# Moving elementwise work between VectorE, ScalarE and GpSimd in a four-layer graph network

## The chip, the cores and the metric

The kernel runs on one core of a Trainium2 chip. A core has a matrix engine (TensorE, "PE" in the profile, its weight loads "PEld"), a vector engine (VectorE, "DVE"), a scalar engine (ScalarE, "ACT"), a third elementwise engine (GpSimd, "POOL") and a queue engine for transfers (SyncE, "SP"). They run side by side, each in the order of its own queue, and wait for each other by semaphores. Matmul results land in PSUM, which has eight banks here, each of 128 partitions by 512 numbers of fp32; everything else lies in SBUF. The metric is the time of the whole kernel on the device, in microseconds (us), as the median of several runs.

## The reference

There are 128 graphs of 64 nodes with 256 features. Four layers follow each other, each of the form `x = layernorm(x + layer(x, adj))`. What matters here is layer 0 (a gated network of five steps), layer 1 (an RMS norm over 1024 hidden features) and the layer norm that closes each layer:

```python
def _layernorm(x, axis=-1, eps=1e-5):
    m = jnp.mean(x, axis=axis, keepdims=True)
    v = jnp.var(x, axis=axis, keepdims=True)
    return (x - m) / jnp.sqrt(v + eps)

# layer 0: five gated steps
for l in range(weight.shape[0]):
    m = jnp.einsum('bnd,de->bne', h, weight[l])
    agg = jnp.einsum('bij,bid->bjd', A, m)
    h = _gru_cell(agg, h, w_ih, w_hh, b_ih, b_hh)      # r, z, n gates, then (1 - z) * n + z * h

# layer 1: hidden features with an RMS norm
agg = epsilon * x + neighbor_sum
h = jnp.einsum('bnd,dh->bnh', agg, W1) + b1
var = jnp.mean(jnp.square(h), axis=-1, keepdims=True)
h = jax.nn.silu(h * jax.lax.rsqrt(var + eps) * rms_weight)
out = jnp.einsum('bnh,hd->bnd', h, W2) + b2
# layers 2 and 3: a hyperbolic map and an attention over adj
```

## The kernel before

The kernel works on 16 groups of 8 graphs. Two graphs share the 128 partitions, so a group is four blocks (`NB = 4`) of 128 rows. Three groups' buffers exist (`NF = 3`), and a small list scheduler written in Python interleaves the groups: each operation is recorded with an engine, an expected duration and what it reads and writes, and is then issued in an order that keeps the engines busy under those durations. The scheduler runs while the program is built; on the chip each engine just works down its queue. All of it is fp32, and the trace shows each fp32 matmul of the program as two instructions (transposes as one).

One gated step works on the group's two halves `n = 0, 1`, each 128 partitions by 2 x 256. It uses the differences between the halves, so that the products of the second half are built from those of the first:

```python
def aggregate(dst, src, b0, n):
    ps = bank("ps_agg")
    for j in range(2):
        for c in range(KD):
            pe(128, lambda j=j, c=c: matmul(ps[...], src[:, b0 + j, ...], ed[:, 2 * n + j, :], 0, 1), ...)
    act(512, lambda: nc.scalar.copy(dst[:, :, half(n)], blocks_of(ps.tile())), [(dst, n)], [ps])   # L476

def minus(o, x0, x1, r):                                                                           # L550
    pool(1.32, lambda: nc.gpsimd.tensor_sub(view(o), x0(), x1()), [o], r)

def plus(o, ps, x):                                                                                # L567
    dve(512, lambda: nc.vector.tensor_add(o.tile(), blocks_of(ps.tile()), x.tile()), [o], [ps, x])

def new_n(n, t):
    # L580: t = (t + 1) * hnb          two inputs in SBUF
    # L582: t = p_in + t               one input in PSUM
    # L584: t = tanh(t + bias)         ScalarE
    # L586: hN = h - t                 two inputs in SBUF
def new_state(n, t, z):
    # L590: hN = (z + 1) * hN          L592: hN = 0.5 * hN + t      two inputs in SBUF each

sides(0)                         # aggregate(agg, hr, 0, 0), p_hn, hnb of half 0
... cut: products p1 and p_in of half 0, its gate and new_n(0, ur) ...
sides(1)                         # the same of half 1
minus(t1, of(a, 1), of(a, 0), [a])                                # t1 = agg1 - agg0
minus(t2, of(h, 1), lambda: view(t1), [(h, 1), t1])               # t2 = h1 - t1
minus(t3, of(h, 1), of(a, 1), [(h, 1), (a, 1)])                   # t3 = h1 - agg1
minus(t4, lambda: view(t2), of(h, 0), [t2, (h, 0)])               # t4 = t2 - h0
product(pu, s2[l], k_view(t2), True, True, t2);  plus(uu, pu, uu)
product(pv, s3[l], k_view(t3), True, False, t3); plus(uv, pv, uu)
product(pw, s1[l], k_view(t1), True, False, t1)
product(pv, na22, k_view(t4), False, True, t4)
plus(uv, pw, uv)
plus(uz, pv, uu)
... cut: the gates' tanh, new_state(0), new_n(1), new_state(1) ...
```

`t1` and `t2` are the two halves of a tile that the trace calls tA, `t3` and `t4` those of tB; `a` is the aggregate in SBUF (agg in the trace), `h` the state (hT), and `uu`, `uz`, `uv`, `ur` are the tiles U, Z, V, R. The matmuls of `product` have line L482 in the trace, those of `aggregate` and of the later layers L222.

A layer norm collects statistics on VectorE, takes the power -0.5 on GpSimd and scales on VectorE:

```python
def layer_norm(y, tag, name):
    for b in range(NB):
        # L491, L492: bn_stats, bn_aggr of block b into mv (mean, variance)       VectorE
    pool(0.23, ... ve = variance + LN_EPS ...)                                    # L493
    pool(1.04, ... rstd = ve ** -0.5 ...)                                         # L494
    for b in range(NB):
        dve(256, lambda b=b: nc.vector.tensor_scalar(                             # L497
            o[:, b, :], y[:, b, :], mv[:, b, 0:1], rstd[:, b:b + 1], OP.subtract, OP.mult), ...)
```

Layer 1 computes its 1024 hidden features in eight blocks of 128 features by 512 rows, and sums their squares:

```python
for c in range(KH):                                               # 8 blocks
    ps = bank("ps_hid")
    ... cut: two matmuls of 512 columns into ps (L222) ...
    act(512, ... hc = ps + b1 ...)                                # L668, out of PSUM
    pool(1.04, ... sq = hc * hc ...)                              # L671, GpSimd
    if c:
        dve(512, ... sqs = sqs + sq ...)                          # L674
... cut: ps_ss, the power on GpSimd (L681), ps_rms, the gate (L689 to L694), ps_o, layer norm ...
```

Of the kernel before, what the change touches and what calls it, by code (L numbers as in the profile page):

```python
# [14 lines left out]
OP = mybir.AluOpType  # L15
# [134 lines left out]
def kernel(  # L150
# [79 lines left out]
    def dve(n, run, w, r):  # L230
        flow.op("DVE", 0.16 + 0.00105 * n, run, w, r)

    def act(n, run, w, r):
        flow.op("ACT", 0.27 + 0.00077 * n, run, w, r)

    def pool(us, run, w, r=()):
        flow.op("POOL", us, run, w, r)
# [8 lines left out]
    def blocks_of(t):  # L246
        return t.rearrange("p (b d) -> p b d", d=D)
# [175 lines left out]
    def b1c(c):  # L423
        return cols[:, 2 * NV + c:2 * NV + c + 1]
# [7 lines left out]
    def group(g):  # L432
# [9 lines left out]
        def rows(tag, name):  # L442
            return u(tag, name, (P, NB, D))

        def half(n):
            return slice(n * HR, (n + 1) * HR)
# [21 lines left out]
# [5 lines that stand above are left out]
                    pe(128, lambda j=j, c=c: matmul(  # L473
                        ps[:, c * HR + j * P:c * HR + (j + 1) * P], src[:, b0 + j, c * P:(c + 1) * P],
                        ed[:, 2 * n + j, :], 0, 1), [ps], [(src, b0 + j), ed])
            act(512, lambda: nc.scalar.copy(dst[:, :, half(n)], blocks_of(ps.tile())), [(dst, n)], [ps])  # L476

        def product(ps, w, v, first, last, r):

# [7 lines left out]
        def layer_norm(y, tag, name):  # L487
            st, mv = tiny("st", (P, NB, 6)), tiny("mv", (P, NB, 2))
            ve, rstd = tiny("ve"), tiny("rstd")
            for b in range(NB):  # L490
                dve(256, lambda b=b: nc.vector.bn_stats(st[:, b, :], y[:, b, :]), [(st, b)], [(y, b)])  # L491
                dve(4, lambda b=b: nc.vector.bn_aggr(mv[:, b, :], st[:, b, :]), [(mv, b)], [(st, b)])  # L492
            pool(0.23, lambda: nc.gpsimd.tensor_scalar(ve.tile(), mv[:, :, 1], LN_EPS, None, OP.add), [ve], [mv])  # L493
            pool(1.04, lambda: nc.gpsimd.tensor_tensor(rstd.tile(), ve.tile(), m_half, OP.pow), [rstd], [ve])  # L494
            o = rows(tag, f"x_{name}")
            for b in range(NB):
                dve(256, lambda b=b: nc.vector.tensor_scalar(  # L497
                    o[:, b, :], y[:, b, :], mv[:, b, 0:1], rstd[:, b:b + 1], OP.subtract, OP.mult),
                    [(o, b)], [(y, b), mv, rstd])
            return o  # L500

        if g >= 2:
# [18 lines left out]
        def gated(l, h):  # L521
            agg = u("agg", f"agg{l}", (P, KD, R))
            hr = rows("B", f"hr{l}") if l else xt

            hnb = u("y", f"hnb{l}", (P, KD, R))

            def sides(n):

                if l:
                    ps = rows_of(h, n)  # L530
                    act(512, lambda: nc.scalar.copy(hr[:, 2 * n:2 * n + 2, :], blocks_of(ps.tile())),
                        [(hr, 2 * n), (hr, 2 * n + 1)], [ps])
                aggregate(agg, hr, 2 * n, n)
                p_hn = bank("p_hn")
                product(p_hn, w_hn, lambda k: h[:, k, half(n)], True, True, (h, n))
                for c in range(KD):
                    act(300, lambda c=c: nc.scalar.activation(  # L537
                        hnb[:, c, half(n)], p_hn[:, c * HR:(c + 1) * HR], AF.Identity,
                        bias=half_b[:, 2 * KD + c:2 * KD + c + 1], scale=0.5), [(hnb, (n, c))], [p_hn, half_b])

            hN = u("h", f"hT{l}", (P, KD, R))
            tA, tB = (u(i, f"t{i}_{l}", (P, 2 * KD, HR)) for i in "AB")
            t1, t2, t3, t4 = (tA, 0), (tA, 1), (tB, 0), (tB, 1)
            a = agg

            def view(t):
                return t[0][:, t[1] * KD:(t[1] + 1) * KD, :]

            def minus(o, x0, x1, r):
                pool(1.32, lambda: nc.gpsimd.tensor_sub(view(o), x0(), x1()), [o], r)  # L550

            def of(t, n):
                return lambda: t[:, :, half(n)]

            def k_of(t, n):
                return lambda k: t[:, k, half(n)]

            def k_view(t):
                return lambda k: t[0][:, t[1] * KD + k, :]

            p1, pu, pv, pw = bank("p_r0"), bank("p_u"), bank("p_v"), bank("p_w")
            p_in = [bank("p_in"), bank("p_in")]

            uu, uz, uv, ur = (u(t, f"{t}_{l}", (P, KD, HR)) for t in ("ZUVR" if l % 2 else "UZVR"))

            def plus(o, ps, x):
                dve(512, lambda: nc.vector.tensor_add(o.tile(), blocks_of(ps.tile()), x.tile()), [o], [ps, x])  # L567

            def tanh_half(o, src, i, r):
                for c in range(KD):  # L570
                    act(256, lambda c=c: nc.scalar.activation(  # L571
                        o[:, c, :], src(c), AF.Tanh, bias=half_b[:, i * KD + c:i * KD + c + 1], scale=0.5),
                        [(o, c)], [r, half_b])

            def inplace(o):
                return lambda c: o[:, c, :]

            def new_n(n, t):

                dve(512, lambda: nc.vector.scalar_tensor_tensor(  # L580
                    t.tile(), t.tile(), 1.0, hnb[:, :, half(n)], OP.add, OP.mult), [t], [t, (hnb, (n, 0)), (hnb, (n, 1))])
                dve(512, lambda: nc.vector.tensor_add(t.tile(), blocks_of(p_in[n].tile()), t.tile()), [t], [t, p_in[n]])  # L582
                for c in range(KD):
                    act(256, lambda c=c: nc.scalar.activation(t[:, c, :], t[:, c, :], AF.Tanh, bias=bih(2 * KD + c)),  # L584
                        [(t, c)], [(t, c), cols])
                dve(512, lambda: nc.vector.tensor_sub(hN[:, :, half(n)], h[:, :, half(n)], t.tile()), [(hN, n)], [(h, n), t])  # L586

            def new_state(n, t, z):

                dve(512, lambda: nc.vector.scalar_tensor_tensor(  # L590
                    hN[:, :, half(n)], z.tile(), 1.0, hN[:, :, half(n)], OP.add, OP.mult), [(hN, n)], [(hN, n), z])
                dve(512, lambda: nc.vector.scalar_tensor_tensor(  # L592
                    hN[:, :, half(n)], hN[:, :, half(n)], 0.5, t.tile(), OP.mult, OP.add), [(hN, n)], [(hN, n), t])

            sides(0)
            product(p1, a11[l], k_of(a, 0), True, False, (a, 0))
            act(420, lambda: nc.scalar.copy(uu.tile(), blocks_of(p1.tile())), [uu], [p1])
            product(p_in[0], w_in[l], k_of(a, 0), True, True, (a, 0))
            product(p1, a12, k_of(h, 0), False, True, (h, 0))
            tanh_half(ur, lambda c: p1[:, c * HR:(c + 1) * HR], 0, p1)  # L600
            new_n(0, ur)
            sides(1)

            minus(t1, of(a, 1), of(a, 0), [a])
            minus(t2, of(h, 1), lambda: view(t1), [(h, 1), t1])
            minus(t3, of(h, 1), of(a, 1), [(h, 1), (a, 1)])
            minus(t4, lambda: view(t2), of(h, 0), [t2, (h, 0)])
            product(pu, s2[l], k_view(t2), True, True, t2)  # L610
            plus(uu, pu, uu)
            product(pv, s3[l], k_view(t3), True, False, t3)
            plus(uv, pv, uu)
# [4 lines that stand above are left out]
            product(pw, s4[l], k_of(h, 1), False, True, (h, 1))  # L618
            tanh_half(uz, inplace(uz), 1, uz)
            new_state(0, ur, uz)  # L620
            tanh_half(uv, inplace(uv), 1, uv)
            plus(uu, pw, uu)
            product(p_in[1], w_in[l], k_of(a, 1), True, True, (a, 1))
            tanh_half(uu, inplace(uu), 0, uu)
            new_n(1, uu)
            new_state(1, uu, uv)
            return hN
# [34 lines left out]
        for c in range(KH):  # L662
            ps = bank("ps_hid")
            for k in range(KD):
# [3 lines left out]
            act(512, lambda ps=ps, hc=hc, c=c: nc.scalar.activation(  # L668
                hc[0][:, hc[1], :], ps.tile(), AF.Identity, bias=b1c(c)), [hc], [ps, cols])
            sq = u("ZR"[c % 2], f"sq{c}") if c else sqs  # L670
            pool(1.04, lambda hc=hc, sq=sq: nc.gpsimd.tensor_mul(sq.tile(), hc[0][:, hc[1], :], hc[0][:, hc[1], :]),  # L671
                 [sq], [hc])
            if c:
                dve(512, lambda sq=sq: nc.vector.tensor_add(sqs.tile(), sqs.tile(), sq.tile()), [sqs], [sqs, sq])  # L674
        ps = bank("ps_ss")
# [190 lines left out]
```

## Time and profile before

The median of three runs is 2712.8 us (2710.44 to 2714.72). One profiled execution had a span of 2704.5 us:

| engine | busy, us | share | instructions |
|---|---|---|---|
| PE (matmul) | 2488.3 | 92% | 11970 |
| DVE | 1675.7 | 62% | 3594 |
| ACT | 1079.3 | 40% | 2371 |
| POOL | 780.8 | 29% | 707 |

The profile gives the busy time of each engine, the waits (an idle stretch before an instruction is put down to the instruction whose end released it), the chain that ended last (followed back from the last instruction, at each step to what released it) and the single instructions in order of time. The end of a matmul is modelled and matmuls overlap in the array, so a busy PE need not be a PE at its peak; the distance between starts says more. The granted TensorE clock is 0.979 of full speed in the mean and lower in the last part of the run, where the last group has the core to itself.

The groups of instructions that the change touches, before:

| line, engine | what | count | mean, ns |
|---|---|---|---|
| L550 POOL | the four differences, 128x512 | 80 each | 1348 to 1465 |
| L671 POOL | squares of a hidden block, 128x512 | 112, and 16 into sqs | 1039, 1088 |
| L497 DVE | scaling of a layer norm, 128x256 | 192 and 64 | 483, 438 |
| L476 ACT | copy of the aggregate out of PSUM, 128x512 | 160 | 578 |
| L668 ACT | hidden block out of PSUM, 128x512 | 128 | 687 |

### The profile page before, as it was taken

Reading aid. Unit: us, or ns where it says so; the run is one execution under the profiler, and the core shown is the slowest. Engines: PE = TensorE matmul, PEld = TensorE weight load, DVE = VectorE, ACT = ScalarE, POOL = GpSimd, SP = SyncE. Lnnn points to the kernel's source line nnn. Section 1 sums busy time; section 2 is a strip of 40 time slices with the busy share of each in tenths; the row PEclk is TensorE's granted clock in tenths of the full one; section 3 lists DMA queues with packets and bytes.
Section 4 is the critical chain, followed back from the end, with each engine's and each line's share of the span. In section 5 each row is a group of like instructions: output and inputs, shape, how many; then the busy total and the mean of one; then the engine's idle time right before and its main releaser. Section 6 shows DMA issues by size and latency. Waiting matters only on the chain.

```text
span 2704.5 us, 32558 instructions
## 1 busy us (share of the span) xinstructions
PE 2488.3 (92%) x11970; PEld 2059.1 (76%) x11970; DVE 1675.7 (62%) x3594; ACT 1079.3 (40%) x2371; POOL 780.8 (29%) x707
## 2 busy tenths in 40 slices
PE   7999998999999899998999989999999999999874
PEld 5887877788787777877788777877777778787743
DVE  2456766676566656656576566765667566576635
ACT  3444433444434344433444334444334443434322
POOL 4224133322413323133322323233233322323220
PEclk9999999999999999999999999999999999999986
DMA  3000000000000000000000000000000000000000
GB/s 116 1 9 1 18 9 15 12 1 26 0 18 8 1 26 1 19 8 18 8 1 26 1 18 8 18 9 1 18 9 18 9 1 26 1 9 8 3 13 8
DMA packets 39150, 35.16 MB, mean 13 GB/s; under 512 B 9892, under 2 KB 38592, under 8 KB 38992
## 3 DMA queue, kind: packets, MB, share of 16 engines
q1 hardware_dynamic: 34848, 28.05, 3.2%
q10 hardware_dynamic: 3744, 4.46, 0.5%
q8 instruction: 95, 1.56, 0.2%
q0 software_dynamic: 400, 0.57, 0.1%
q14 instruction: 63, 0.52, 0.1%
HBM read 24.69 MB, written 8.39 MB: 12 GB/s over the span
## 4 chain that ended last, share of the span: by engine, by line
PE 56%; DVE 21%; POOL 10%; issue 6%; ACT 6%; DMA 0%; POOLq 0%; DVEq 0%; ACTq 0%; SPq 0%
PE ps_hid L222 8%; PE p_v L482 7%; PE ps_o L222 7%; PE p_r L482 7%; PE p_w L482 5%; PE p_in L482 5%; POOL tA L550 4%; PE ps_agg L222 3%; PE p_hn L482 3%; POOL tB L550 3%; PE p_u L482 3%; DVE st L491 2%; PE ps_a L222 2%; DVE x_n L497 2%; DVE hT L590 2%
## 5 line engine op out<-in xcount | busy, mean ns | idle before, releaser
L550 POOL TENSOR_TENSOR tA<-agg 128x512 f32<-128x512 f32 x80 | 107.8, 1348 | 841.9 <-ACT agg L476 738.7
L482 PE MATMUL p_hn<-hT,w_hn 128*128 128x256 f32 x1280 | 323.6, 381 | 0.0
L482 PE MATMUL p_in<-agg,w_in 128*128 128x256 f32 x1280 | 312.5, 380 | 7.6 <-ACT agg L476 7.6
L482 PEld LDWEIGHTS p_in<-agg,w_in 128*128 128x128 f32 x1280 | 241.0, 190 | 41.3 <-ACT agg L476 9.7
L482 PEld LDWEIGHTS p_hn<-hT,w_hn 128*128 128x128 f32 x1280 | 230.0, 192 | 23.7
L222 PE MATMUL ps_o<-w2s,hid 128*128 128x256 f32 x1024 | 231.5, 381 | 3.7 <-DVE hid L694 3.4
L222 PE MATMUL ps_hid<-aggm,w1s 128*128 128x512 f32 x512 | 224.7, 597 | 0.7 <-ACT aggm L476 0.7
L571 ACT ACTIVATE V<-V,half_b 128x256 f32<-128x256 f32 x160 | 73.2, 501 | 377.5 <-DVE V L567 377.5
L222 PEld LDWEIGHTS ps_o<-w2s,hid 128*128 128x128 f32 x1024 | 194.5, 191 | 33.0 <-DVE hid L694 6.3
L482 PE MATMUL p_u<-tA,s 128*128 128x256 f32 x640 | 162.5, 393 | 44.3 <-POOL tA L550 44.2
L674 DVE TENSOR_TENSOR sqs<-sqs,sq 128x512 f32<-128x512 f32 x112 | 77.5, 692 | 180.0 <-POOL sq L671 180.0
L222 PEld LDWEIGHTS ps_hid<-aggm,w1s 128*128 128x128 f32 x512 | 97.7, 192 | 118.2 <-issue 114.4
L482 PE MATMUL p_v<-tB,na 128*128 128x256 f32 x640 | 163.9, 396 | 25.1 <-DVE V L567 24.8
L482 PEld LDWEIGHTS p_u<-tA,s 128*128 128x128 f32 x640 | 119.4, 194 | 78.1 <-POOL tA L550 60.9
L482 PE MATMUL p_w<-tA,s 128*128 128x256 f32 x640 | 162.6, 381 | 0.0
L482 PEld LDWEIGHTS p_v<-tB,na 128*128 128x128 f32 x640 | 123.6, 198 | 50.4 <-DVE V L567 16.8
L482 PE MATMUL p_r<-agg,a 128*128 128x256 f32 x640 | 156.1, 381 | 6.1 <-ACT agg L476 6.0
L482 PE MATMUL p_r<-hT,a 128*128 128x256 f32 x640 | 159.4, 379 | 0.0
L537 ACT ACTIVATE hnb<-p_hn,half_b 128x256 f32<-128x256 f32 x320 | 134.2, 469 | 62.5 <-PE p_hn L482 61.3
L482 PE MATMUL p_w<-hT,s 128*128 128x256 f32 x640 | 159.0, 380 | 0.0
L580 DVE SCALAR_TENSOR_TENSOR R<-R,hnb 128x512 f32<-128x512 f32 x80 | 65.0, 812 | 143.7 <-ACT R L571 143.3
L482 PE MATMUL p_v<-tB,s 128*128 128x256 f32 x640 | 153.9, 379 | 0.0
(192 smaller groups left out, 4932.5 us busy)
## 6 DMA issues: line engine op xcount, KB each, us to landing
x<-in_x_dram SPq DMA_DIRECT2D x16, 512.0 KB, 3.7
xr<-in_x_dram SPq DMA_DIRECT2D x16, 512.0 KB, 3.3
out_dram<-x_n SPq DMA_DIRECT2D x16, 512.0 KB, 2.9
edge<-in_adj_dram SPq DMA_DIRECT2D x32, 64.0 KB, 2.3
wm<-in_L_gnn_weight_dram ACTq DMA_DIRECT2D x5, 256.0 KB, 8.9
w1s<-in_L_gnn_W_dram ACTq DMA_DIRECT2D x1, 1024.0 KB, 11.7
w2s<-in_L_gnn_W_dram ACTq DMA_DIRECT2D x1, 1024.0 KB, 8.4
aw_in_L_gnn_w_ih_dram<-in_L_gnn_w_ih_dram ACTq DMA_DIRECT2D x1, 512.0 KB, 5.6
```

Source lines behind the costliest of these rows:

```text
L222: nc.tensor.matmul(o, lhsT, rhs, start=(k == 0), stop=(k == nk - 1))
L482: pe(256, lambda c=c, k=k: nc.tensor.matmul(ps[:, c * HR:(c + 1) * HR], w[:, k, c * P:(c + 1) * P], v(k), start=first and c == k == 0, sto ...
L491: dve(256, lambda b=b: nc.vector.bn_stats(st[:, b, :], y[:, b, :]), [(st, b)], [(y, b)])
L497: dve(256, lambda b=b: nc.vector.tensor_scalar(o[:, b, :], y[:, b, :], mv[:, b, 0:1], rstd[:, b:b + 1], OP.subtract, OP.mult), [(o, b)], [ ...
L537: act(300, lambda c=c: nc.scalar.activation(hnb[:, c, half(n)], p_hn[:, c * HR:(c + 1) * HR], AF.Identity, bias=half_b[:, 2 * KD + c:2 * K ...
L550: pool(1.32, lambda: nc.gpsimd.tensor_sub(view(o), x0(), x1()), [o], r)
L571: act(256, lambda c=c: nc.scalar.activation(o[:, c, :], src(c), AF.Tanh, bias=half_b[:, i * KD + c:i * KD + c + 1], scale=0.5), [(o, c)], ...
L580: dve(512, lambda: nc.vector.scalar_tensor_tensor(t.tile(), t.tile(), 1.0, hnb[:, :, half(n)], OP.add, OP.mult), [t], [t, (hnb, (n, 0)), ( ...
L590: dve(512, lambda: nc.vector.scalar_tensor_tensor(hN[:, :, half(n)], z.tile(), 1.0, hN[:, :, half(n)], OP.add, OP.mult), [(hN, n)], [(hN, ...
L674: dve(512, lambda sq=sq: nc.vector.tensor_add(sqs.tile(), sqs.tile(), sq.tile()), [sqs], [sqs, sq])
```

## The change

Three kinds of elementwise work change engines. The differences of the gated steps go from GpSimd to VectorE, and the two that use the second half's aggregate read it from its PSUM bank rather than from the copy that ScalarE makes. The squares of layer 1 go from GpSimd to ScalarE, which reads the hidden block's PSUM bank a second time (the square of the same sum with the bias). Of each layer norm's four scalings two go from VectorE to ScalarE, as `rstd * y + off`, for which VectorE computes `off = -mean * rstd` in one small instruction. GpSimd keeps the powers, a bias sum per group and little else. The purpose is to take GpSimd out of the gated steps' path and to use idle ScalarE time. The scheduler's expected durations change with it, so the order of instructions changes on every engine.

```diff
@@ aggregate, sides
+            return ps                       # aggregate hands out its bank
-                aggregate(agg, hr, 2 * n, n)
+                p_agg = aggregate(agg, hr, 2 * n, n)
+                return p_agg                # so does sides
@@ layer_norm
+            off = tiny("off")
+            dve(4, lambda: nc.vector.scalar_tensor_tensor(
+                off.tile(), mv[:, :, 0], -1.0, rstd.tile(), OP.mult, OP.mult), [off], [mv, rstd])
             for b in range(NB):
-                dve(256, lambda b=b: nc.vector.tensor_scalar(
-                    o[:, b, :], y[:, b, :], mv[:, b, 0:1], rstd[:, b:b + 1], OP.subtract, OP.mult),
-                    [(o, b)], [(y, b), mv, rstd])
+                if b % 2:
+                    act(300, lambda b=b: nc.scalar.activation(
+                        o[:, b, :], y[:, b, :], AF.Identity, bias=off[:, b:b + 1], scale=rstd[:, b:b + 1]),
+                        [(o, b)], [(y, b), off, rstd])
+                else:
+                    dve(240, lambda b=b: nc.vector.tensor_scalar(
+                        o[:, b, :], y[:, b, :], mv[:, b, 0:1], rstd[:, b:b + 1], OP.subtract, OP.mult),
+                        [(o, b)], [(y, b), mv, rstd])
@@ gated
             def minus(o, x0, x1, r):
-                pool(1.32, lambda: nc.gpsimd.tensor_sub(view(o), x0(), x1()), [o], r)
+                dve(512, lambda: nc.vector.tensor_sub(view(o), x0(), x1()), [o], r)
...
-            sides(1)
+            p_a2 = sides(1)
+            a2 = lambda: blocks_of(p_a2.tile())
-            minus(t1, of(a, 1), of(a, 0), [a])
+            minus(t1, a2, of(a, 0), [p_a2, (a, 0)])
             minus(t2, of(h, 1), lambda: view(t1), [(h, 1), t1])
-            minus(t3, of(h, 1), of(a, 1), [(h, 1), (a, 1)])
+            minus(t3, of(h, 1), a2, [(h, 1), p_a2])
             minus(t4, lambda: view(t2), of(h, 0), [t2, (h, 0)])
@@ layer 1
             sq = u("ZR"[c % 2], f"sq{c}") if c else sqs
-            pool(1.04, lambda hc=hc, sq=sq: nc.gpsimd.tensor_mul(sq.tile(), hc[0][:, hc[1], :], hc[0][:, hc[1], :]),
-                 [sq], [hc])
+            act(512, lambda ps=ps, sq=sq, c=c: nc.scalar.activation(sq.tile(), ps.tile(), AF.Square, bias=b1c(c)),
+                [sq], [ps, cols])
```

## The prediction

> **What bounds the kernel now.** I read the page's first part, then the chain, then the waits of TensorE, then stretches of the run, and last one stretch instruction by instruction.
>
> The page (time in us, share of the span, number of instructions; the second line is the chain that ended last, by engine):
>
> ```profile
> PE 2488.3 (92%) x11970; PEld 2059.1 (76%) x11970; DVE 1675.7 (62%) x3594; ACT 1079.3 (40%) x2371; POOL 780.8 (29%) x707
> PE 56%; DVE 21%; POOL 10%; issue 6%; ACT 6%; DMA 0%; POOLq 0%; DVEq 0%; ACTq 0%; SPq 0%
> ```
>
> TensorE is the bound. How far from its own limit is it? Its "busy" is too generous, because the ends of matmuls are modelled, so I take the distance from start to start in runs without a gap. In the chain, 40 matmuls of ps_o (256 columns) take 8.65 us, 0.216 each; 32 of ps_hid (512 columns) take 13.73 to 13.9, 0.433 each; 128 columns or a transpose come to half of 0.216, 0.108. Counted by shape in the grouped instructions there are 552 of 512 columns, 8616 of 256 or 257 and 2802 small ones: 239 + 1864 + 304 = 2407 us. Of the span of 2704.5 some 297 us is therefore not matmul streaming, and no change on the other engines can win more than that. Where does it lie? Stretches of the run (length; busy us and count of each engine; TensorE clock; DMA):
>
> ```profile
> 0.00:100.00 100.00, 85.60 (x404) 68.34 (x405) 30.71 (x57) 33.53 (x79) 38.57 (x43) 1.00 0.25 78
> 1000.00:1400.00 400.00, 375.45 (x1795) 310.64 (x1794) 250.91 (x538) 163.35 (x359) 122.03 (x109) 0.99 0.03 9
> 2500.00:2600.00 100.00, 83.54 (x380) 69.25 (x378) 59.25 (x149) 33.46 (x79) 22.20 (x22) 0.93 0.03 11
> 2600.00:2705.00 105.00, 55.25 (x176) 37.35 (x176) 48.98 (x148) 21.52 (x44) 18.93 (x22) 0.70 0.02 5
> ```
>
> Priced as above, the first 100 us lose 18 (10 of them the first loads), the last 205 us lose about 90, because the last group of molecules runs almost alone, and 100 to 2500 loses about 190 in many small gaps. The gaps by what ended them (us in total, times, longest):
>
> ```profile
> PE p_u L482 <- POOL tA L550: 44.2, 37, 3.6
> PE ps_hr L463 <- DVE hT L592: 27.4, 18, 4.5
> PE p_v L482 <- DVE V L567: 24.8, 19, 4.2
> PE ps_sup L222 <- DVE tan L743: 24.1, 7, 9.9
> PE ps_agg L222 <- DVE x_n L497: 18.9, 16, 3.8
> ```
>
> The largest is the wait of p_u for the difference t2 that GpSimd makes; the next four are waits for VectorE results. Now the same stretch on GpSimd and on VectorE (start, duration, instruction):
>
> ```profile
> 1059.62 1.27 POOL L550 TENSOR_TENSOR tA<-agg 128x512 f32<-128x512 f32 x1 [4.90 <-ACT agg L476]
> 1060.85 1.72 POOL L550 TENSOR_TENSOR tB<-hT,agg 128x512 f32<-128x512 f32 x1
> 1062.53 1.72 POOL L550 TENSOR_TENSOR tA<-hT,tA 128x512 f32<-128x512 f32 x1
> ```
>
> ```profile
> 1058.37 0.69 DVE L580 SCALAR_TENSOR_TENSOR R<-R,hnb 128x512 f32<-128x512 f32 x1
> 1059.70 1.74 DVE L580 SCALAR_TENSOR_TENSOR R<-R,hnb 128x512 f32<-128x512 f32 x1
> 1061.54 0.69 DVE L582 TENSOR_TENSOR R<-p_in,R 128x512 f32<-128x512 f32 x1
> 1062.15 2.65 DVE L586 TENSOR_TENSOR hT<-hT,R 128x512 f32<-128x512 f32 x2
> ```
>
> The same L580 takes 0.69 us while GpSimd is idle and 1.74 us beside a GpSimd subtraction; L582, which has one input in PSUM, keeps its 0.69. GpSimd's subtractions stretch too, from 1.27 to 1.72.
>
> **What the Trainium skill says.** "SBUF — State Buffer", section "Who interferes with whom": a VectorE instruction with two SBUF inputs shares a read path with GpSimd instructions that read SBUF, and whichever issues second fully blocks. The trace agrees. Adding up, for each VectorE form, the time over its undisturbed duration, I find 201 instructions that overlap an L550 subtraction and lose 127 us, and none that loses time to the squares (L671), to the powers of the norms or to an instruction with a PSUM input. "VectorE: DVE Perf Modes", section "The perf-mode tier table": a two-input fp32 instruction runs in the plain mode whether its source is SBUF or PSUM. The trace agrees: 0.69 us either way. "ScalarE: Activation LUTs", section "What ACT_TABLE_LOAD costs": each [128,1] pointer operand of an ACTIVATE adds about 93 ns. The trace has no instruction with both scale and bias as pointers over a whole tile; with the bias alone one over 256 columns takes 0.50, so my estimate for the new norm instruction is 0.59.
>
> **The change, part by part.**
>
> 1. Differences. 5 layers x 16 groups x 4 = 320 subtractions leave GpSimd (1.35 to 1.47 mean, 449 us in all) and become VectorE instructions of 0.69: +220 us on VectorE. Two of four read the aggregate from PSUM, so the first needs no ScalarE copy. Path from the last aggregate matmul to p_u before: copy 0.58, then t1, t3, t2 (GpSimd's order in the trace) at 1.27, hops about 0.3: 4.7 us undisturbed, 5.8 in the stretch above. After: hop 0.25, t1, one foreign VectorE instruction that the built program mostly puts between, t2, at 0.69 less 0.08 overlap each, hop: about 2.2. In the built program of before, TensorE has mostly 4.3 to 6.1 us of other matmuls between these two points, about what the path needs, hence the gaps; in the changed one mostly 3.0, so 0.8 to spare.
> 2. Blocking. With L550 gone from GpSimd the 127 us go as well.
> 3. Norms. 128 of the 256 scalings (mean 0.48, of which 0.41 is undisturbed) leave VectorE: -52 us without counting the blocking twice. 64 small instructions for the offset come: 64 x 0.165 = +11. ScalarE gets 128 x 0.59 = +76. Per norm: before 4 x 0.41 = 1.64; after 0.2 for the offset, then two on each engine, 1.2 on ScalarE, so 0.2 to 0.4 sooner.
> 4. Squares. 128 leave GpSimd (1.04, 134 us) and become ScalarE instructions out of PSUM at about 0.69, as the L668 copy from the same bank: +88. In this stage ScalarE then needs 2 x 0.69 = 1.38 us per block where TensorE needs 4 x 0.433 = 1.73: not the bound, but 80% of ScalarE for 14 us per group.
>
> Sums: VectorE 1676 + 220 - 127 - 52 + 11 = about 1728 (before 1676). ScalarE 1079 + 76 + 88 = about 1243. GpSimd 781 - 449 - 134 = about 198. So a large job moves to VectorE at a net cost of only 50 us.
>
> On the path that sets the end I price the gaps of TensorE: p_u 44 to about 8 (-36); p_v 25 to 14 (-11; both programs leave about 3.0 us there, but VectorE is no longer blocked); ps_hr 27 to 13 (-14; L586, L590 and L592 all have two SBUF inputs); ps_agg after a norm 19 to 13 (-6); ps_sup 24 to 18 (-6). That is -73. Each gap also costs more than its idle time, since the pipe refills (p_u means 393 ns against 381 elsewhere, and the sum of the gaps that have an entry is smaller than the 190 not streamed): -18 more. End and start, where the last group's chain is shorter by 2 to 3 us in each of its last two layers: -6. New waits from a fuller ScalarE and VectorE: +12. Total -85: 2712.8 - 85 = **2628 us**.
>
> **The rivals.**
>
> (a) VectorE's queue becomes the wait. It works in order; the differences now stand in it behind other groups' instructions, and its mean load stays at about 65%. For: three of the five large gaps already wait for VectorE, and the changed order is packed closer (3.0 against 4.3 to 6.1 us). Against: blocking goes. If this wins, the p_u gap stays under another name: 2680 to 2720.
>
> (b) ScalarE holds the bank of the hidden layer twice as long and delays the tanh of the other groups in that stage. For: 11 of 14 us. Against: 46% mean load, 1.38 under 1.73. Cost if it bites: 1 to 3 us per group, 2645 to 2675.
>
> (c) The gaps were mostly due to the scheduler's plan not being met, since it prices instructions as if nothing were blocked. Then taking the blocking away lets all of it run as planned, and the middle falls to what 100 to 400 us shows (about 4% lost, not 8%): another -30, 2590 to 2600.
>
> **Range and chances.** Centre 2628; (a) pulls up and (c) down: 2580 to 2678 holds it 8 times in 10. The line of 2% is at 2658.5, 30 us above my centre, where a standard deviation of about 37 leaves three chances in four below it; slower by over 2% would need rival (a) at its worst plus a new stall.
>
> **What would show it.** VectorE busy near 1730, L580, L586, L590, L592 all near 0.69 mean; GpSimd near 200; ScalarE near 1240; the wait of p_u for tA under 10 us; TensorE's streamed sum unchanged, as the count of matmuls is. I am wrong if TensorE shows long waits for tA from VectorE (rival a), if ps_hid shows gaps for ScalarE (rival b), or if L580 and its like stay stretched.

## The result, and the profile after

The changed kernel takes 2585.4 us (median of four runs, 2585.0 to 2586.9) against 2712.3 us before: a ratio of 0.953, with a 95% interval of 0.952 to 0.955. It is 127 us faster; the prediction said 85 us, with 2580 to 2678 as its range. (The profiled execution of the changed kernel has a span of 2582.9 us, that of before 2704.5.) Line numbers move by about ten: L550 becomes L560, L567 L577, L580 to L592 L590 to L602, L497 L506, and L502 is the new ScalarE half of the norm.

The page of the changed kernel, its first line and its chain:

```profile
PE 2447.7 (95%) x11970; PEld 2051.2 (79%) x11970; DVE 1711.6 (66%) x3850; ACT 1222.8 (47%) x2627; POOL 200.4 (8%) x259
PE 63%; DVE 19%; ACT 5%; POOL 2%; issue 2%; DMA 1%; POOLq 0%; ACTq 0%; DVEq 0%; SPq 0%
```

The matmuls are the same 11970, GpSimd has all but left the chain (10% to 2%), and VectorE is only 36 us busier although it took over 220 us of subtractions (it also gave up half of the norms' scalings). Stretches of the run (length, busy time and count of each engine):

```profile
0.00:100.00 100.00, 88.36 (x414) 71.48 (x415) 35.19 (x67) 35.57 (x84) 27.67 (x35) 1.00 0.25 78
1000.00:1400.00 400.00, 390.14 (x1953) 332.87 (x1952) 278.04 (x645) 195.92 (x429) 27.48 (x38) 1.00 0.04 12
2478.00:2583.00 105.00, 54.01 (x177) 37.52 (x176) 48.35 (x147) 31.00 (x61) 10.63 (x14) 0.72 0.03 10
```

The counts can be compared: in the same 400 us of the middle TensorE now gets through 1953 matmuls instead of 1795. The last 105 us are as before (177 matmuls against 176). So the gain lies in the middle. The waits of TensorE:

```profile
PE ps_e L815 <- DVE junk_d L810: 20.3, 15, 1.5
PE ps_agg L222 <- DVE x_n L506: 19.7, 14, 3.8
PE ps_hr L463 <- DVE hT L602: 16.1, 9, 4.8
PE p_r L483 <- ACT agg L476: 14.2, 15, 1.5
PE ps_sup L222 <- DVE tan L754: 10.7, 1, 10.7
...
PE p_u L483 <- DVE tA L560: 4.9, 3, 2.5
...
PE p_v L483 <- DVE V L577: 0.8, 1, 0.8
```

p_u fell from 44.2 to 4.9 and p_v from 24.8 to 0.8. The waits of TensorE in all come to 124.6 us, against 205.2 before. And the VectorE instructions that GpSimd had stretched (busy us, mean ns), two of them before and then four after:

```profile
L586 DVE TENSOR_TENSOR hT<-hT,R 128x512 f32<-128x512 f32 x80 | 78.9, 987 | 20.7 <-ACT R L584 20.1
L580 DVE SCALAR_TENSOR_TENSOR R<-R,hnb 128x512 f32<-128x512 f32 x80 | 65.0, 812 | 143.7 <-ACT R L571 143.3
```

```profile
L596 DVE TENSOR_TENSOR hT<-hT,R 128x512 f32<-128x512 f32 x80 | 56.9, 711 | 27.3 <-ACT R L594 27.3
L600 DVE SCALAR_TENSOR_TENSOR hT<-V,hT 128x512 f32<-128x512 f32 x80 | 55.1, 689 | 1.5
L590 DVE SCALAR_TENSOR_TENSOR R<-R,hnb 128x512 f32<-128x512 f32 x80 | 54.7, 684 | 99.0 <-ACT R L581 99.0
L560 DVE TENSOR_TENSOR tB<-tA,hT 128x512 f32<-128x512 f32 x80 | 75.3, 941 | 0.5
```

Before, the first three of the four had means of 987, 772 and 812 ns; all are at their undisturbed 0.69 us now, but for a few of the first. The fourth is a new difference, and its mean of 941 shows that a little blocking is left; it is looked at below. Added up over every VectorE form as in the prediction, but for all GpSimd instructions, VectorE was blocked for 142 us before and for 23 after. In the trace of before all of the 142 fall into overlaps with the subtractions of L550, so the 127 of the prediction came out some 15 us short.

### The profile page after: what moved, and what is told of

It is laid out like the page before. It is cut to its first block, busy times and chain, and to the rows that moved or that the text cites. A ratio compares the mean times of both kernels' runs of the same rounds, so it can differ in the third digit from the quotient of the medians.

```text
span 2582.9 us, 32405 instructions
## 1 busy us (share of the span) xinstructions
PE 2447.7 (95%) x11970; PEld 2051.2 (79%) x11970; DVE 1711.6 (66%) x3850; ACT 1222.8 (47%) x2627; POOL 200.4 (8%) x259
## 4 chain that ended last, share of the span: by engine, by line
PE 63%; DVE 19%; ACT 5%; POOL 2%; issue 2%; DMA 1%; POOLq 0%; ACTq 0%; DVEq 0%; SPq 0%
PE ps_hid L222 9%; PE ps_o L222 8%; PE p_v L483 7%; PE p_r L483 7%; PE p_w L483 7%; PE p_hn L483 7%; PE p_in L483 6%; PE ps_agg L222 5%; PE p_u L483 3%; DVE st L492 2%; DVE hT L600 1%; POOL rstd L495 1%; DVE junk_d L810 1%; PE ps_hr L463 1%; DVE tA L560 1%
## 5 line engine op out<-in xcount | busy, mean ns | idle before, releaser
L483 PE MATMUL p_r<-agg,a 128*128 128x256 f32 x640 | 157.4, 382 | 14.2 <-ACT agg L476 14.2
L483 PE MATMUL p_u<-tA,s 128*128 128x256 f32 x640 | 154.5, 380 | 4.9 <-DVE tA L560 4.9
L483 PE MATMUL p_v<-tB,na 128*128 128x256 f32 x640 | 154.4, 379 | 0.8 <-DVE V L577 0.8
L540 ACT COPY hr<-ps_hr 128x512 f32<-128x512 f32 x128 | 74.8, 585 | 145.8 <-PE ps_hr L463 145.8
L483 PEld LDWEIGHTS p_r<-agg,a 128*128 128x128 f32 x640 | 116.9, 190 | 31.6 <-ACT agg L476 18.1
L222 PEld LDWEIGHTS ps_agg<-edge,hr 128*128 128x128 f32 x1024 | 133.2, 192 | 6.4 <-ACT hr L540 0.7
L483 PEld LDWEIGHTS p_v<-tB,s 128*128 128x128 f32 x640 | 121.4, 190 | 21.1 <-issue 5.3
```

Source lines behind the costliest of these rows:

```text
L222: nc.tensor.matmul(o, lhsT, rhs, start=(k == 0), stop=(k == nk - 1))
L483: pe(256, lambda c=c, k=k: nc.tensor.matmul(ps[:, c * HR:(c + 1) * HR], w[:, k, c * P:(c + 1) * P], v(k), start=first and c == k == 0, sto ...
```

## The experiments

The theory under test: GpSimd's subtractions blocked VectorE, and freeing it is what shortens the waits of TensorE. The rivals: the path from the aggregate to p_u is shorter; the scheduler found a better order; the norms and squares relieve VectorE and GpSimd. All times are medians (of 4 runs, for norm_only of 12 and for dummy_same of 5), with their ratio to the kernel before on the same chip:

| run | what | us | ratio, 95% interval |
|---|---|---|---|
| diff_only | differences on VectorE, two out of PSUM | 2682.8 | 0.988, 0.987 to 0.990 |
| diff_sbuf | the same out of SBUF | 2613.3 | 0.963, 0.961 to 0.965 |
| norm_only | half of each norm on ScalarE | 2714.3 | 1.000, 0.999 to 1.001 |
| sq_only | squares on ScalarE | 2737.8 | 1.009, 1.007 to 1.010 |
| old_plan | diff_sbuf in (nearly) the order of before | 2577.9 | 0.950, 0.948 to 0.952 |
| new_plan_pool | differences on GpSimd, planned as on VectorE | 2741.5 | 1.010, 1.008 to 1.013 |
| dummy_two | changed kernel, GpSimd subtracts to no purpose | 2751.0 | 1.014, 1.011 to 1.016 |
| dummy_same | changed kernel, GpSimd squares to no purpose | 2691.8 | 0.992, 0.989 to 0.994 |
| old_plan_dummy | old_plan with dummy_two's subtractions | 2786.6 | 1.027, 1.025 to 1.028 |
| old_plan_psum | old_plan, two differences out of PSUM | 2565.6 | 0.945, 0.944 to 0.947 |
| all_old_plan | old_plan with norms and squares | 2573.4 | 0.948, 0.947 to 0.949 |
| slack | diff_sbuf, differences planned longer | 2621.8 | 0.966, 0.965 to 0.968 |

### The parts one at a time

diff_only takes the difference hunks of the change alone; diff_sbuf leaves out their PSUM half:

```diff
 def minus(o, x0, x1, r):
-    pool(1.32, lambda: nc.gpsimd.tensor_sub(view(o), x0(), x1()), [o], r)
+    dve(512, lambda: nc.vector.tensor_sub(view(o), x0(), x1()), [o], r)
```

> Only the differences change: VectorE, two of them out of PSUM; norms and squares as before. If the gain is that GpSimd no longer blocks VectorE, nearly all of it is here: 2600 to 2620 us, with L580, L586, L590 and L592 at 0.69 us mean. If the three parts share the gain: 2640 to 2660.

> As diff_only, but t1 and t3 read the aggregate from the ScalarE copy in SBUF. If the path from the aggregate to p_u matters, the copy of 0.58 us in front of it costs 80 x 0.3 to 0.6: 25 to 45 us over diff_only. If blocking is the cause, within 8 us of diff_only, as VectorE runs the same number of equally long instructions.

Both expectations missed. diff_only gained 31 us and not 94 to 114, although it did what the theory says to VectorE: its trace has the instructions of L580 to L592 back at 0.69 us (only R<-R,hnb keeps a mean of 0.79) and 23 us of blocking left. diff_sbuf, whose instructions take as long and whose path has the ScalarE copy in front, is 70 us faster than diff_only. Neither the length of the path nor blocking can give that sign and size. What differs besides is the order, which the scheduler makes anew for each kernel (and the reading of PSUM, which is tested below). The waits of diff_only show no single cause:

```profile
PE ps_hr L463 <- DVE hT L594: 34.8, 24, 4.9
PE ps_sup L222 <- DVE tan L746: 24.9, 6, 9.9
PE ps_agg L222 <- DVE x_n L498: 23.5, 10, 3.7
```

p_u is not among them (its wait for tA is 4.8 us): TensorE is short of work at the ends of steps and layers.

norm_only and sq_only take one of the other hunks each:

> Only the norms change. VectorE loses about 60 us of work, half of it time in which it was blocked. Blocking theory: the cause stays, -5 to -15 us (2698 to 2708). If VectorE's load was the cause: -25 to -40.

> Only the squares change. In the trace of before the squares blocked nothing and little waited for them. Expected 2705 to 2720; if the queue of GpSimd (the differences standing behind squares) was a cause, 2680 to 2695.

The norms alone change nothing, the squares alone cost 0.9%; neither time lies in the range expected. In sq_only the wait of p_u for GpSimd's differences rises from 44 to 74 us, although GpSimd has 134 us less to do:

```profile
PE p_u L482 <- POOL tA L550: 73.8, 47, 4.3
PE ps_T L453 <- DVE x_n L497: 44.2, 15, 9.2
```

In its built program 12 of the 80 gated steps leave TensorE at most 0.6 us of other matmuls between the aggregate and p_u (before, the least is 1.3), where the path takes 4.7: the order again.

But the waits of TensorE as a whole did not rise: they come to 206 us against 205 before, because others fell. What rose is the time at a low clock. The mean granted clock is 0.963 against 0.979. In the trace of before the clock is at half ten times between 100 and 2500 us, for 3.4 us or more, and each time a wait of TensorE of 1.4 to 4.6 us lies next to it. Eight matmuls behind such a wait, and eight elsewhere:

```profile
1271.19 3.37 PE L482 MATMUL p_u<-tA,s 128*128 128x256 f32 x8 [3.62 <-POOL tA L550]
1019.25 1.89 PE L482 MATMUL p_v<-tB,s 128*128 128x256 f32 x8
```

At half clock the matmuls of 256 columns start 0.427 us apart instead of 0.216. Adding up what each matmul that starts at half clock loses, I estimate the loss at 36 us before, 76 in sq_only, 47 in diff_only and 15 in the changed kernel. That is more than enough for the 24 us of sq_only. No run tests whether the waits bring the half clock on.

Taken one by one the parts win 31, 0 and -24 us, and together 127, so they do not add up: single hunks could not be judged without holding the order still.

### The order held still

The scheduler orders by the engine and duration given when an operation is recorded, while the instruction that runs is free. old_plan gives it GpSimd and 1.32 us, and runs the difference on VectorE; new_plan_pool does the reverse:

```diff
 def minus(o, x0, x1, r):       # old_plan
-    pool(1.32, lambda: nc.gpsimd.tensor_sub(view(o), x0(), x1()), [o], r)
+    pool(1.32, lambda: nc.vector.tensor_sub(view(o), x0(), x1()), [o], r)
 def minus(o, x0, x1, r):       # new_plan_pool
-    pool(1.32, lambda: nc.gpsimd.tensor_sub(view(o), x0(), x1()), [o], r)
+    dve(512, lambda: nc.gpsimd.tensor_sub(view(o), x0(), x1()), [o], r)
```

> The kernel before, with the differences run on VectorE out of the SBUF copies, but planned by the scheduler as if they were GpSimd instructions of 1.32 us: TensorE's order is that of before but for a few swaps. Blocking theory: blocking is gone, so most of the gain comes, 2600 to 2640. Theory that the new order makes the gain: 2690 or more.

> The reverse: the kernel before, with the differences on GpSimd as before, but planned as VectorE instructions of 0.70 us. The order leaves them too little time. Blocking theory and path theory: slower than before, 2720 to 2800. Theory that the order alone makes the gain: under 2690.

old_plan is 136 us faster than before with TensorE's order all but unchanged (6421 of the program's 6554 matmuls stand at the same place), which is more than expected, and faster than the changed kernel. The new order is not what makes the gain. new_plan_pool adds that an order made for short differences costs 28 us when they are long. It also makes a second pair: diff_sbuf has the same recorded operations and nearly the same order (6471 of 6554), and is 128 us faster. So running the differences on VectorE instead of GpSimd wins 136 us in one order and 128 in the other. The waits of old_plan, with nearly the same order as before, can be compared one by one:

```profile
PE ps_hr L463 <- DVE hT L592: 13.5, 11, 4.5
PE ps_sup L222 <- DVE tan L743: 12.7, 4, 9.9
...
PE ps_agg L222 <- DVE x_n L497: 6.8, 8, 3.8
...
PE p_u L482 <- DVE mv L492: 5.0, 4, 1.3
PE p_v L482 <- DVE V L567: 3.9, 5, 1.0
```

p_u went from 44.2 to 5.0 (and 0.2 more, for tA itself): the path, in which some blocking is hidden, since the subtractions took 1.35 to 1.47 us in the mean and 1.27 undisturbed. The other four went from 27.4 + 24.1 + 18.9 + 24.8 = 95.2 to 36.9 us, with 220 us more work on VectorE; blocking had stretched or held up the instructions that these waits end with. By these waits about 40% of what was won is the path and 60% the rest. That split is read from who ended the waits; no run separates the two cleanly, and in the rest is also that GpSimd comes to its powers sooner (VectorE waited 212 us for them before, 94.0 of it in the scalings of the norms, and 131 in old_plan, 59.7 of it there).

### Blocking put back

dummy_two and dummy_same keep the changed kernel's order on the other engines, since the extra instruction hangs on the same recorded operation:

```diff
 def minus(o, x0, x1, r):
-    dve(512, lambda: nc.vector.tensor_sub(view(o), x0(), x1()), [o], r)
+    def both():
+        nc.vector.tensor_sub(view(o), x0(), x1())
+        nc.gpsimd.tensor_sub(junk_p, view(o), w_hn)        # dummy_two
+        nc.gpsimd.tensor_mul(junk_p, view(o), view(o))     # dummy_same, in its place
+    dve(512, both, [o], r)
```

> The changed kernel, and behind each of the 320 differences on VectorE a GpSimd subtraction of the same size, of the new difference and a constant tile, whose result nobody reads (extra work, nothing is left out). The order on TensorE, VectorE and ScalarE is that of the changed kernel. Blocking theory: VectorE is blocked again, 100 to 130 us of it come back in L590 to L602, and the time rises by 50 to 100 us to 2635 to 2685. Theory of the shorter path or of the better order: these stay, so at most +15 us, 2585 to 2600.

> The control: the same, but the GpSimd instruction multiplies the new difference by itself, as the squares of before did, which lost VectorE nothing in 6 overlaps. Its queue on GpSimd is as full as in dummy_two (320 x 1.04 against 1.26 us). If only the two different operands block, 2585 to 2595. If any GpSimd instruction that reads SBUF blocks a VectorE instruction with two SBUF inputs, as for dummy_two.

old_plan_dummy puts the same subtraction into old_plan.

> old_plan, and behind each difference on VectorE the GpSimd subtraction of dummy_two, which nobody reads. TensorE keeps the order of before, the differences themselves stay short, only the blocking is back. Blocking theory: nearly all of the 136 us of old_plan are lost again, 2690 to 2740. Path theory (the differences took 1.27 us each in a row, now 0.69): most of it stays, 2580 to 2620. A result near 2650 says half and half.

All three lose more than the change had won, or most of it: +166, +106 and +209 us, by work whose results nobody reads. dummy_two and old_plan_dummy even end above the ranges of the blocking theory. TensorE's order is that of the changed kernel in the first two, matmul by matmul, and that of old_plan but for 10 of 6554 in the third. With the same instructions VectorE's busy time rises from 1711.6 us to 1908.9 and 1860.4, and from 1714.6 to 1943.6. The stretched instructions in dummy_two:

```profile
L562 DVE TENSOR_TENSOR tA<-hT,tA 128x512 f32<-128x512 f32 x80 | 91.6, 1145 | 0.4
L606 DVE SCALAR_TENSOR_TENSOR hT<-hT,R 128x512 f32<-128x512 f32 x80 | 77.7, 971 | 1.0
L562 DVE TENSOR_TENSOR tB<-hT,ps_agg 128x512 f32<-128x512 f32 x80 | 54.1, 676 | 0.0
L524 DVE TENSOR_SCALAR edge<-edge 64x256 f32<-64x256 f32 x32 | 46.5, 1454 | 0.5
```

tA<-hT,tA (t2, two SBUF inputs) rose from 685 to 1145 ns, while tB<-hT,ps_agg (t3, one input in PSUM) stays at 676 a moment later beside the same GpSimd work. And p_v, at 0.8 us in the changed kernel, waits again (35.7 us in dummy_two, 56.3 in old_plan_dummy). One sentence of my expectation for old_plan_dummy was wrong: the differences do not stay short. t2 and t4 follow the first dummy and are blocked by it, at 1.23 us, so blocking lengthens the path too, and this run cannot tell the theories apart as cleanly as it meant to. It does show that such GpSimd work, with nothing else changed, costs more than the whole change brings. And dummy_same, meant as the control, blocks too, so no run has large GpSimd work that does not block: that the loss comes from blocking rests on the stretched instructions and on the waits behind them.

Set side by side with the blocked time of VectorE, by order of instructions (for the dummies, what is blocked without them and the rise of the busy time):

```
order of before:        blocked 1 us   2577.9 (old_plan)
                        blocked 142    2713   (before)
                        blocked 230    2786.6 (old_plan_dummy)
order of the change:    blocked 23     2585.4 (changed kernel)
                        blocked 172    2691.8 (dummy_same)
                        blocked 220    2751.0 (dummy_two)
```

In one order 0.9 to 1.0 us of time goes with each us blocked, in the other 0.7 to 0.8 (differences to the first row of each; the row of before also has the longer path). Between orders the blocked time ranks nothing: sq_only, with about 88 us blocked, is slower than before, and diff_only, with 23, takes 2682.8. The dummies also fill GpSimd's queue before its powers, so part of these slopes may be that; but VectorE waits for the powers 164 us in the changed kernel and 175 and 171 in its two dummies, 131 in old_plan and 137 in old_plan_dummy, which leaves it little.

### Reading PSUM, the other two parts, and slack

old_plan_psum reads t1 and t3 from the bank; all_old_plan adds the norm and square hunks to old_plan; slack is diff_sbuf with the differences recorded at 1.0 us.

```diff
-minus(t1, of(a, 1), of(a, 0), [a])                     # old_plan_psum
+minus(t1, a2, of(a, 0), [p_a2, a])
-minus(t3, of(h, 1), of(a, 1), [(h, 1), (a, 1)])
+minus(t3, of(h, 1), a2, [(h, 1), p_a2, (a, 1)])
-dve(512, lambda: nc.vector.tensor_sub(view(o), x0(), x1()), [o], r)              # slack
+flow.op("DVE", 1.0, lambda: nc.vector.tensor_sub(view(o), x0(), x1()), [o], r)
```

> old_plan, but t1 and t3 read the aggregate out of its PSUM bank as in the change; still planned as 1.32 us each. If reading PSUM is what made diff_only 70 us slower than diff_sbuf (the ScalarE copy of the aggregate waited 21.8 us for the differences in the trace of the changed kernel), 20 to 70 us over old_plan: 2600 to 2650. If that was only the order that the scheduler found, within 12 us of old_plan: 2566 to 2590.

> old_plan with the norms and squares of the change. If these two help once VectorE is free: 2550 to 2570, under both kernels. If they only mattered through the order: 2570 to 2590, as the changed kernel and old_plan.

> diff_sbuf, with the differences planned at 1.0 us on VectorE rather than 0.70, so that the order leaves more TensorE work between the aggregate and p_u (mean 6.8 us against 6.2 in diff_sbuf and 4.9 in old_plan). If too tight a plan is what sets diff_sbuf 35 us behind old_plan: 2570 to 2595. If the orders differ by chance: anywhere from 2590 to 2640.

old_plan_psum takes 2565.6 us, the best time here, 20 us under the changed kernel:

```profile
PE 2452.4 (96%) x11970; PEld 2046.9 (80%) x11970; DVE 1717.8 (67%) x3914; ACT 1082.0 (42%) x2371; POOL 342.8 (13%) x387
```

Reading PSUM therefore isn't what slows diff_only. The two kernels run the same instructions, each as long but for 20 us of blocking (23 us in diff_only, 3 in old_plan_psum), and stand 117 us apart by order. (Its order is not exactly that of old_plan, since the bank is held longer, so its 12 us over old_plan may be order as well.) all_old_plan is 4.5 us under old_plan, near the noise: norms and squares on ScalarE bring next to nothing there, though its order differs from that of old_plan as well. slack was expected to help and did not: 8 us slower than diff_sbuf. How much TensorE work stands between the aggregate and p_u does not by itself rank the orders, and what makes one order good stays open.

## Why the prediction was right, point by point

**The bound and the part that could be won.** Right. The streamed matmuls come to the same 2407 us; of the 297 us beside them the change took 122. The end of the run kept its losses, where I had counted on 6 us from start and end.

**Part 1 and 2, the sums of the engines.** VectorE 1711.6 (1728 predicted), ScalarE 1222.8 (1243), GpSimd 200.4 (198). The new norm instruction on ScalarE takes 594 ns, 0.59 predicted. VectorE's blocked time fell by 119 us, where I had counted on 127; the bias sum xb still blocks.

**The gaps, where the size was off.** Predicted: p_u to 8, p_v to 14, ps_hr to 13, ps_agg to 13, ps_sup to 18, new waits +12. Measured: 4.9, 0.8, 16.1, 19.7, 10.7, and ps_e 20.3 (2.0 before) and p_r 14.2 (6.0) as the new ones, +26. The waits as a whole fell by 80.6 us; my terms gave 61. The five terms fell by 87 us where I had 73, and the new waits took back 14 more than I had: the two errors cancel. The missing 20 us lie in small waits that I did not price, such as p_in (7.6 before, 0.7 now) and ps_agg for edge (6.3, 1.3) and for hnb (4.8, none). Of the five, p_v is the most wrong: I let half of it stand because both programs leave 3.0 us there. The slack was enough: old_plan, with almost the old order, waits 3.9 us, and dummy_two brings 35.7 back. The norm's wait (ps_agg) did not get shorter in the changed kernel, and no experiment says why.

**The cost of a gap beyond its idle time.** This is the largest mis-sized term, and my reason for it, that the pipe refills, was not the main one. I gave it 18 us. The span fell by 121.6 us for 80.6 us of waits, so it was 41. By the estimate above some 21 of these are matmuls that no longer run at half clock (36 us before, 15 now), which the prediction did not look at; the other 20 stay open. The profile of before had the ratio in plain sight: 297 us not streamed for 205 us of waits, 1.45. Scaling the predicted 61 us by it would have given 88 rather than 79 for the two terms. But it is no constant: from before to old_plan the span changed by 1.3 us for one of waits, from the changed kernel to dummy_two by 1.8, and sq_only has a longer span without more waits.

**The rivals.** (a) did not come: TensorE waits 4.9 us for VectorE's differences, and VectorE at 66% carries them. (b) did not come: the waits of TensorE list no ps_hid but one of 0.7 us. (c) describes what happened best: priced as in the prediction, the matmuls leave 4.1% of the time between the first 100 and the last 205 us unused, against 8.4% before, as it said, and its 2590 to 2600 us is the nearest figure. But it is only half true, because the plan that is met without blocking is not the better plan: old_plan, planned as if the differences still took 1.32 us on another engine, beats it.

**What the prediction missed.** I treated the order as a detail that the change brings with it. Between orders of the same instructions the runs differ by 117 us (diff_only and old_plan_psum) and by 35 (diff_sbuf and old_plan), as much as the change itself. That the changed kernel came out well is partly luck of its order: with the differences alone the same scheduler's order gave 31 us.

## What to carry to other kernels

Before giving GpSimd elementwise work, look in the trace for VectorE instructions with two SBUF inputs, or of the plain scale-and-add kind, whose mean is well over their minimum: time that GpSimd "takes over" may come back as blocked VectorE time. Here 449 us of GpSimd work raised VectorE's busy time by only 39 us in old_plan (1675.7 to 1714.6), where nothing else moved. When a scheduler orders the program, test a change once with the order held still (same recorded engine and duration, another instruction) before judging its parts. And expect a wait of TensorE to cost more than its idle time: compare the time not streamed with the waits, and look at the granted clock behind the long ones.

## What the runs showed of the hardware that was not expected

A GpSimd product of a tile with itself blocks VectorE as well. In the trace of before, six overlaps with the squares had lost nothing, and I took that for a rule. But in all six the VectorE instruction had started first, and in two of them it was the square that took longer, 1.44 us instead of 1.04 (GpSimd, then VectorE):

```profile
848.00 1.44 POOL L671 TENSOR_TENSOR sqs<-hid 128x512 f32<-128x512 f32 x1 [4.27 <-ACT hid L668]
```

```profile
847.85 0.69 DVE L592 SCALAR_TENSOR_TENSOR hT<-hT,R 128x512 f32<-128x512 f32 x1
```

In dummy_same the same form makes VectorE 149 us busier than in the changed kernel, and t2 has a mean of 1025 ns instead of 685. Small GpSimd instructions did no such harm: in old_plan 16 VectorE instructions with two SBUF inputs start during one on 128x4, and all keep 0.68 or 0.69 us.

A VectorE instruction with a single SBUF tensor blocks too. The 64x256 scaling of edge (L523 in the changed kernel) takes 283 ns undisturbed, 965 in the kernel before and 1347 and 1454 in the dummies. The Trainium skill has this ("SBUF — State Buffer", section "Who interferes with whom"): tensor_scalar can enter a mode that uses both port pairs. I had quoted that section for two-input instructions only.

One GpSimd instruction is left in the way. The bias sum xb takes 2.46 us, once per group, and it meets t4 (start, duration, instruction; first GpSimd, then VectorE, of the changed kernel):

```profile
1118.91 2.46 POOL L667 TENSOR_TENSOR xb<-x_n,b_r 128x1024 f32<-128x1024 f32 x1 [2.40 <-ACT x_n L502]
```

```profile
1119.07 0.68 DVE L560 TENSOR_TENSOR tB<-hT,ps_agg 128x512 f32<-128x512 f32 x1
1119.66 2.25 DVE L560 TENSOR_TENSOR tB<-tA,hT 128x512 f32<-128x512 f32 x1
1121.84 0.60 DVE L523 TENSOR_SCALAR edge<-edge 64x256 f32<-64x256 f32 x2
```

t3 beside it, with an input in PSUM, keeps 0.68 us; t4 takes 2.25. The differences carry 20 of the 23 us still blocked. In old_plan_psum, where the order keeps them apart, 3 us are left. Moving xb elsewhere was not tried.
